# The last stage of a four-stage network: where the preparation of the last 512 tokens is placed, and which engine makes the low parts of the split operands

## The chip, the cores and the metric

The kernel runs on one core of one Trainium2 chip. A core has five engines with instruction queues of their own that run in order: PE (matrix multiplications), DVE and ACT (elementwise work over 128 partitions), POOL (elementwise work too) and SP, which here only starts transfers. Engines wait for each other by semaphores. The metric is the device time of one execution in microseconds (us); lower is better. Times are medians of several runs. The profile is that of one execution.

## The reference

`x` has 2 x 1024 tokens of 128 features. Four residual stages follow each other, each on a normalised `x`: an attention with 16 heads of 8, a mixture of 8 experts with two chosen, a causal attention with 8 heads of 128, and a mixture of 16 experts with four chosen. The change touches only the last one:

```python
t = x * rsqrt(mean(x * x) + EPS) * scale
g = t @ gate_w.T + gate_b
vals, idx = top_k(g, 4);  w = softmax(vals)          # route[e]: the weight of expert e, 0 if not chosen
for each expert e of 16:
    h = t @ w1[e].T + b1[e]                          # 128 -> 256, even outputs are x_glu, odd ones x_lin
    s = min(x_glu, 7) * sigmoid(1.702 * x_glu) * (clip(x_lin, 7, 7) + 1)
    acc += route[e] * (s @ w2[e].T + b2[e])
return x + acc
```

The clip has equal bounds, so its factor is always 8 and only the even outputs are needed. All 16 experts are computed for all tokens, and the route weights (mostly zero) scale their results.

## The kernel before

The 2048 tokens are worked on as four chunks of 512 (`c` = 0 to 3), with features on the partitions: a tile is 128 x 512 float32. The first three stages fill the time up to about 877 us. The last stage is made of two generators, whose `yield`s mark the points where the builder may change over to other work.

`ffn1_front(c)` (L989 to L1036) is the preparation of one chunk, in 16 pieces: statistics and inverse roots on DVE, the normalised tokens `f1tt` and `f1xl` (L1004, eight DVE operations), an addition into `x` on POOL (L1008), a transposition on PE, a scaled copy on ACT (L1012), the split of the transposed tokens into two parts (`f1x`), the gate's matmuls (L1019), four rounds of top-4 on small DVE tiles (L550 to L560), an exponential on ACT (L1025), the normalised route weights (up to L570), their transposition, and a store of them to DRAM (L1034), from which they are later loaded back broadcast over the partitions.

`ffn1_back(c)` (L1038 to L1084) are the 16 experts of one chunk. For expert `e`:

- three matmuls make `p` in PSUM (`mm3`, L161: high by high, high by low, low by high part, for near float32 precision); `pu` has four buffers,
- ACT applies the activation, into `f` (L1063), of which there are five buffers,
- DVE takes the minimum and multiplies with the broadcast route weight `gb` (L1064, called the scaling below); `gb` comes by a transfer that SP starts (L1048) and has eight buffers,
- `split` makes two parts of `f` for the next matmul: the high part is a rounding cast on ACT (L158), the low part the difference `f` minus high part (L159), on POOL or on DVE, by the expert's number (L1069),
- seven experts behind (`LAG`), three matmuls add the expert's result to `y` in PSUM.

After the sixteenth expert, `y` is copied, transposed, added to `x` (`res`, L1082) and stored (L1083).

The low parts go to POOL where `d % 5` is 1 or 3: experts 1, 3, 6, 8, 11 and 13 of a chunk, 6 of 16. The preparation of the first three chunks lies in the stage before. That of the last chunk runs with the experts of chunk 0: one piece after each expert (L1185). Chunk 1 follows alone, then chunks 2 and 3.

The order in which this program is written is not yet the order on the engines. Outside a part of the first stage the framework lays the instructions out with a planner, which walks a timeline with its own costs and reorders within each engine's queue; so the preparation's small DVE operations are found between the scalings of the experts, and some of them earlier or later than written. The final queues are fixed when the program is built, and each engine runs its queue in order. In the queues of this kernel, the eight normalisations of chunk 3 stand behind the scaling of expert 9 of chunk 0 on DVE, its top-4 rounds begin before the scaling of expert 15 of chunk 0, and its last small operation (L570) stands behind the scaling of expert 0 of chunk 2. POOL's addition (L1008) stands between the low parts of experts 8 and 11 of chunk 0.

Of the kernel before, what the change touches and what calls it, by code (L numbers as in the profile page):

```python
# [38 lines left out]
def cols(t, w=128):  # L39
    return slice(t * w, (t + 1) * w)  # L40


def run(*gens):
    for g in gens:
        for _ in g:
            pass
# [26 lines left out]
class Net:  # L73
# [964 lines left out]
    def ffn1_back(self, c, wk, pu, out):  # L1038
        nc = self.nc
        E = 16  # L1040
        LAG, PO = 7, (1, 3)
        F7 = 7.0 / (1.0 + math.exp(-1.702 * 7.0))
        xh, gT, gd = self.f1st.pop(c)
        gbs = []

        def bcast(e):
            gb = wk.tile([128, CH], F32, tag="f1gb", name=f"f1gb_{c}_{e}", bufs=8)
            nc.sync.dma_start(out=gb, in_=gd[e : e + 1, :].to_broadcast([128, CH]))  # L1048
            gbs.append(gb)

        for e in range(4):
            bcast(e)
        y = self.psy.tile([128, CH], F32, tag="y", name=f"f1y_{c}")
        nc.tensor.matmul(y, lhsT=self.f1b2, rhs=gT, start=True, stop=False)
        hs = []
        for e in range(E + LAG):
            if e + 4 < E:
                bcast(e + 4)
            if e < E:
                p = pu.tile([128, CH], F32, tag="u", name=f"f1p_{c}_{e}")  # L1060
                self.mm3(p, [w[:, e, :] for w in self.f1w1], xh)
                f = wk.tile([128, CH], F32, tag="f", name=f"f1f_{c}_{e}", bufs=5)
                nc.scalar.activation(f, p, AF.Gelu_apprx_sigmoid, bias=self.f1b1[:, e : e + 1])  # L1063
                nc.vector.scalar_tensor_tensor(f, f, F7, gbs[e], ALU.min, ALU.mult)  # L1064
                hs.append(f)
            d = e - 1
            if 0 <= d < E:
                fs = [wk.tile([128, CH], F32R, tag=f"fs{k}", name=f"f1s{k}_{c}_{d}", bufs=8) for k in range(2)]
                self.split(fs, hs[d], nc.gpsimd if d % 5 in PO else nc.vector)  # L1069
                hs[d] = fs  # L1070
            d = e - LAG
            if d >= 0:
                self.mm3(y, [w[:, d, :] for w in self.f1w2], hs[d], start=False, stop=d == E - 1)
            yield
        yT = wk.tile([128, CH], F32, tag="f1yT", name=f"f1yT_{c}")
        nc.scalar.copy(yT, y)
        yield
        tp = self.pt([128, TPC, D], f"f1ytp_{c}")
        for t in range(TPC):
            nc.tensor.transpose(tp[:, t, :], yT[:, cols(t)], self.ident)  # L1080
        res = self.tok.tile([128, TPC, D], F32, tag="xl", name=f"res_{c}")
        nc.vector.tensor_add(res, self.x[c], tp)  # L1082
        nc.sync.dma_start(out=out[c], in_=res)  # L1083
        yield  # L1084


def interleave(main, *sides, ratio=1):
    s = Side()
    for g in sides:
        s.add(g)  # L1090
    for _ in main:
        s.step(ratio)
    s.drain()


def held(net, gen):
    while True:
        with ExitStack() as ctx:
            for ins in net.marks.values():
                ctx.enter_context(net.tc.issue_after(ins.ins))  # L1100
            if next(gen, gen) is gen:
                return
        yield


def later(gen, n):
    for _ in range(n):
        yield
    yield from gen


def build(tc, aps, upto=4):
    n = Net(tc, aps)
    out = aps["out"].rearrange("(c t p) d -> c p t d", p=128, t=TPC)

    def dump():
        for c in range(NCHUNK):
            tc.nc.sync.dma_start(out=out[c], in_=n.x[c])

    with ExitStack() as ctx:  # L1120
        n.setup(ctx)
        c1 = ctx.enter_context(ExitStack())
        cr = ctx.enter_context(ExitStack())
        n.f0wp = n.pool(cr, "f0w")
        w1 = n.attn1_weights(c1)
        with ExitStack() as c0:
            cb = c0.enter_context(ExitStack())
            n.attn0(
                c0, cb,
                {170: lambda: n.ffn0_front(0), 270: lambda: n.ffn0_front(1), 266: lambda: w1,  # L1130
                 394: lambda: n.ffn0_front(2)}
                if upto > 1 else {},
            )
        if upto == 1:
            return dump()
        n.attn1_pools(c1)
        xh = [n.attn1_x(0), None]
        first, g = n.attn1_proj(0, 0, xh[0])
        n.f0k = n.pool(cr, "f0k", 1)
        gens = {"proj": islice(g, 5)}  # L1140
        for c in range(NCHUNK):
            gens[f"front{c}"] = n.ffn0_front(c)
            gens[f"up{c}"] = n.ffn0_up(c)
            gens[f"down{c}"] = n.ffn0_down(c)
        for i in range(2):
            gens[f"a1{i}"] = n.attn1_front(0, xh[0], i)
        with ExitStack() as c0:
            n.psu = n.pool(c0, "f0u", 4, PSUM)
            for word in ORDER.split():
                count, k = word.split("*")  # L1150
                for _ in range(int(count)):
                    next(gens[k], None)
            for k in gens:
                if k not in ("front0", "front1", "front2"):
                    run(gens[k])
            n.psu = None
            n.early = False
        with ExitStack() as c2:
            with ExitStack() as c3:
                n.a1s = n.pool(c3, "a1s", 3, PSUM)  # L1160
                n.a1o = n.pool(c3, "a1o", 1, PSUM)

                def front1():
                    xh[1] = n.attn1_x(1)
                    yield from n.attn1_front(1, xh[1], 0)
                    yield from n.attn1_front(1, xh[1], 1)

                def weights1():
                    cr.close()
                    n.f1wp = n.pool(c2, "f1w")  # L1170
                    yield from n.ffn1_weights()

                plan = {10: [lambda: held(n, front1())]}
                if upto > 3:
                    plan[9] = [lambda: held(n, weights1())]
                    plan[18] = [lambda: n.ffn1_front(0)]
                    plan[21] = [lambda: n.ffn1_front(1)]
                    plan[30] = [lambda: later(n.ffn1_front(2), 3)]
                n.attn1(first, g, xh, plan)
            c1.close()  # L1180
            if upto == 3:
                return dump()
            wk1 = n.pool(c2, "f1k", 2)
            pu = n.pool(c2, "f1u", 4, PSUM)
            interleave(n.ffn1_back(0, wk1, pu, out), n.ffn1_front(3), ratio=1)  # L1185
            run(n.ffn1_back(1, wk1, pu, out))
            run(n.ffn1_back(2, wk1, pu, out), n.ffn1_back(3, wk1, pu, out))


def layout(inputs):  # L1190
# [63 lines left out]
```

## Time and profile before

| | us |
|---|---|
| median of three runs (lowest, highest) | 992.36 (988.16, 992.86) |
| the profiled execution's own time | 993.87 |
| its span, first to last instruction | 992.1 |
| busy over the span: PE, DVE, ACT, POOL | 951.8, 839.4, 597.3, 317.3 |
| first matmul of the last stage's experts begins at | 877.6 |
| first scaling (L1064), last low part (L159) begin at | 882.6, 985.2 |
| 64 scalings on DVE, median of one | 0.680 |
| 40 low parts on DVE, median of one | 0.681 |
| 24 low parts on POOL, median of one | 1.299 |
| 64 activations on ACT, median of one | 0.684 |
| 64 high parts (casts) on ACT, median of one | 0.621 |
| granted TensorE clock over the span | 0.964 |

A row of the profile's groups names a line, an engine, an operation and its tiles, written from output to input, with a count and durations in ns. DVE and ACT start the next operation a little before the last one's recorded end, so an operation of 0.68 us takes up about 0.60 us of its engine. A row of a timeline begins with the start and the duration; several equal instructions in a row are put together with an "x" count; in brackets stands how long the engine had been idle, and what ended that. `f1f` is the activation's tile, `f1s` the split's two parts, `f1p` and `f1y` the two matmuls' results, `f1gb` the route weights.

### The profile page before, as it was taken

The page shows a single profiled execution, that of the slowest core. Times are in us where ns is not written, and L with a number is a line of the kernel's source. Part 1 is how long each engine was busy: PE and PEld are TensorE (multiplying, and loading weights), DVE is VectorE, ACT ScalarE, POOL GpSimd, SP SyncE. Part 2 cuts the span into 40 slices and gives each one's busy share as a digit, 9 for nine tenths or more (in the row PEclk, how much of TensorE's full clock was granted, in tenths as well). Part 3 has the DMA queues.
Part 4 walks back from the last instruction along what each step waited for, and adds up shares of the span by engine and source line. Part 5 has one row for each costly group of instructions (what it writes and reads, how often), then busy time and mean ns, then how long its engine had stood idle before and what let it go on. Part 6 is the DMA issues. An engine that isn't in the chain of part 4 may idle for free.

```text
span 992.1 us, 17673 instructions
## 1 busy us (share of the span) xinstructions
PE 951.8 (96%) x6546; PEld 616.8 (62%) x6546; DVE 839.4 (85%) x1885; ACT 597.3 (60%) x1149; POOL 317.3 (32%) x402
## 2 busy tenths in 40 slices
PE   5999999999999999999989999999999999998997
PEld 4643444444444434447767887788778789876675
DVE  7879789999988888526788897989999978989886
ACT  3157778888887776864435455444444544477775
POOL 7000300000010000002546557554645555336332
PEclk8989899999998978979999999999999999999999
DMA  5520231000200000013100001000000001144462
GB/s 171 191 75 2 99 116 55 2 2 22 80 20 26 2 1 2 2 33 118 44 2 12 22 12 54 23 12 12 12 1 24 12 13 33 33 142 156 151 192 74
DMA packets 33640, 50.94 MB, mean 51 GB/s; under 512 B 5141, under 2 KB 11250, under 8 KB 33554
## 3 DMA queue, kind: packets, MB, share of 16 engines
q1 hardware_dynamic: 33042, 49.68, 15.7%
q8 instruction: 51, 0.84, 0.3%
q14 instruction: 35, 0.29, 0.1%
q0 software_dynamic: 512, 0.13, 0.1%
HBM read 40.00 MB, written 9.67 MB: 50 GB/s over the span
## 4 chain that ended last, share of the span: by engine, by line
PE 62%; DVE 28%; ACT 4%; issue 4%; DMA 1%; SPq 1%; POOL 1%; DVEq 0%; ACTq 0%; POOLq 0%
PE av L415 9%; DVE mx L362 9%; PE o L878 8%; PE st L395 8%; PE st L845 7%; PE av L422 3%; PE s L804 3%; PE st L852 3%; PE f1y L163 2%; PE hot L474 2%; DVE pm L810 2%; PE f1p L163 2%; PE f0y L674 2%; PE s L357 2%; DVE pt L855 2%
## 5 line engine op out<-in xcount | busy, mean ns | idle before, releaser
L362 DVE TENSOR_REDUCE mx<-s 128x2 f32<-128x1024 f32 x256 | 301.5, 1218 | 33.5 <-PE s L357 29.0
L401 ACT ACTIVATE pt<-st 128x512 f32<-128x512 f32 x472 | 253.9, 598 | 69.3 <-PE s L357 54.6
L415 PE MATMUL av<-pt,V 128*32 128x256 f32 x2048 | 170.6, 414 | 0.0
L357 PE MATMUL s<-KS,QM 24*128 24x512 f32 x512 | 154.9, 511 | 7.2 <-DVE mx L362 5.3
L395 PE MATMUL st<-QM,KS 25*128 25x512 f32 x472 | 154.8, 511 | 3.8 <-ACT pt L401 2.3
L878 PE MATMUL o<-V,pt 128*128 128x129 f32 x1152 | 156.8, 277 | 0.3 <-ACT pt L857 0.3
L878 PEld LDWEIGHTS o<-V,pt 128*128 128x128 f32 x1152 | 146.7, 191 | 12.4 <-issue 3.9
L845 PE MATMUL st<-Q,K 128*128 128x512 f32 (+1 forms) x480 | 133.2, 389 | 5.5 <-DVE rB_q L747 3.6
L395 PEld LDWEIGHTS st<-QM,KS 25*128 25x128 f32 x472 | 66.9, 187 | 101.1 <-ACT pt L401 45.6
L857 ACT ACTIVATE pt<-pt 128x512 f32<-128x512 f32 x92 | 53.9, 592 | 73.8 <-DVE pt L855 73.8
L810 DVE TENSOR_REDUCE pm<-s 128x1 f32<-128x512 f32 (+3 forms) x160 | 80.8, 522 | 16.9 <-PE s L804 16.1
L845 PEld LDWEIGHTS st<-Q,K 128*128 128x128 f32 x480 | 78.8, 189 | 17.4 <-DVE rB_q L747 4.9
L415 PEld LDWEIGHTS av<-pt,V 128*32 128x32 f32 x2048 | 43.9, 112 | 69.2 <-issue 66.6
L857 ACT ACTIVATE pt<-st 128x512 f32<-128x512 f32 x68 | 37.5, 551 | 66.3 <-PE st L852 56.0
L357 PEld LDWEIGHTS s<-KS,QM 24*128 24x128 f32 x512 | 64.9, 187 | 20.0 <-DVE mx L362 14.2
L448 POOL TENSOR_TENSOR x<-x,ov 128x128 f32<-128x128 f32 x16 | 7.6, 472 | 194.5 <-DVE ov L443 194.5
L804 PE MATMUL s<-K,Q 128*128 128x512 f32 (+2 forms) x192 | 66.8, 380 | 1.1 <-DVE m L816 1.0
L891 POOL TENSOR_TENSOR x<-x,w 128x128 f32<-128x128 f32 x128 | 59.5, 465 | 24.9 <-ACT w L889 20.6
L855 DVE TENSOR_TENSOR pt<-st,mb 128x512 f32<-128x512 f32 x92 | 57.5, 632 | 5.1 <-PE st L845 1.3
L163 PE MATMUL f1y<-f1s,f1w 128*128 128x512 f32 x192 | 55.9, 412 | 5.1 <-POOL f1s L159 3.0
L889 ACT ACTIVATE w<-o,rz 128x128 f32<-128x128 f32 x128 | 39.9, 364 | 34.6 <-DVE rz L885 26.8
L377 POOL DMA_DIRECT2D QM<-mts x16 | 9.5, 592 | 158.4 <-ACT mts L376 157.7
(224 smaller groups left out, 1636.8 us busy)
## 6 DMA issues: line engine op xcount, KB each, us to landing
f1gb<-f1gd SPq DMA_DIRECT2D x64, 256.0 KB, 3.6
mb<-md SPq DMA_DIRECT2D x17, 256.0 KB, 3.2
f0gb<-f0gd SPq DMA_DIRECT2D x32, 128.0 KB, 3.0
qd<-q SPq DMA_DIRECT2D x12, 256.0 KB, 3.0
kd<-k SPq DMA_DIRECT2D x12, 256.0 KB, 3.0
QM<-qd SPq DMA_DIRECT2D x3, 1024.0 KB, 5.7
KS<-kd SPq DMA_DIRECT2D x2, 1024.0 KB, 6.8
KS<-kd SPq DMA_DIRECT2D x2, 768.0 KB, 8.0
```

Source lines behind the costliest of these rows:

```text
L163: self.nc.tensor.matmul(out, lhsT=lhs[l], rhs=rhs[r], start=start and i == 0, stop=stop and i == 2)
L357: self.last_s = nc.tensor.matmul(ps[:, k, :], lhsT=QM[c][r, g, cols(t)], rhs=KS[c // 2][r, g, cols(h, CH)], start=True, stop=True)
L362: self.marks["V"] = nc.vector.tensor_reduce(mxs[n][:, h, 2 * pr : 2 * pr + 2, t : t + 1], ps, AX.X, ALU.max, negate=True)
L395: nc.tensor.matmul(ps, lhsT=KS[c // 2][32 * j : 32 * j + 25, g, cols(kt)], rhs=QM[c][32 * j : 32 * j + 25, g, :], start=True, stop=True,)
L401: self.marks["A"] = nc.scalar.activation(e, ps, AF.Exp, scale=INV_SQRT_D)
L415: return nc.tensor.matmul(avs[n][cols(j, 32), q], lhsT=V[c // 2][kt // 4][:, kt % 4, 4 * g + j, :], rhs=es[j][:, q], start=kt == 0 and i = ...
L804: nc.tensor.matmul(s[:, 0 : k1 - k0], lhsT=Q[0][:, h, cols(qt)], rhs=K[0][:, k0:k1], start=True, stop=True)
L810: nc.vector.tensor_reduce(pm, s[:, 0:w], AX.X, ALU.max)
L845: k = nc.tensor.matmul(o, lhsT=K[l][:, cols(kt)], rhs=Q[r][:, :, q0 : q0 + w], start=i == 0, stop=apart and i == 2)
L855: nc.vector.tensor_sub(e[:, :, 256 - w :], o, mv)
L857: k = nc.scalar.activation(e[:, :, 256 - w :], o, AF.Exp, scale=INV_SQRT_D)
L878: nc.tensor.matmul(acc[t][:, h, :], lhsT=e[:, h, cols(t)], rhs=V[:, kt, h, :], start=(kt == 0 and h == 0), stop=(kt == qt and h == 1),)
```

## The change

Two edits, both in the last stage. The low parts alternate: those of the odd experts go to POOL, those of the even ones stay on DVE (8 and 8 of 16 in each chunk). And the preparation of chunk 3 no longer takes one piece per expert of chunk 0, but one piece after every third step of chunks 0 and 1; both have 25 steps, so the 16 pieces are used up in chunk 1 (`run` at the end finds none left).

```diff
     def ffn1_back(self, c, wk, pu, out):
...
-        LAG, PO = 7, (1, 3)
+        LAG = 7
...
-                self.split(fs, hs[d], nc.gpsimd if d % 5 in PO else nc.vector)
+                self.split(fs, hs[d], nc.gpsimd if d % 2 else nc.vector)
...
-            interleave(n.ffn1_back(0, wk1, pu, out), n.ffn1_front(3), ratio=1)
-            run(n.ffn1_back(1, wk1, pu, out))
-            run(n.ffn1_back(2, wk1, pu, out), n.ffn1_back(3, wk1, pu, out))
+            front3 = n.ffn1_front(3)
+            for c in range(2):
+                for k, _ in enumerate(n.ffn1_back(c, wk1, pu, out)):
+                    if k % 3 == 2:
+                        next(front3, None)
+            run(front3, n.ffn1_back(2, wk1, pu, out), n.ffn1_back(3, wk1, pu, out))
```

In the queues of the changed program, the eight normalisations of chunk 3 stand behind the scaling of expert 8 of chunk 0, its top-4 rounds begin before the scaling of expert 9 of chunk 1, and L570 stands behind the scaling of expert 2 of chunk 2. POOL's addition L1008 stands between the low parts of experts 7 and 9 of chunk 0. The addition of chunk 0's result (L1082) moves ahead, from behind the scaling of expert 4 of chunk 2 to behind that of expert 7 of chunk 1; its store (L1083), on SP, moves from behind the load of `gb` for expert 12 of chunk 2 to ahead of the first load for chunk 2. The store of chunk 3's route weights (L1034) moves from behind the load for expert 12 of chunk 2 to behind that for expert 14.

## The prediction

> **What bounds the kernel now.** The change lies in the last stage, so I read that stage alone. First the busy time by stretch, cut where the chain of work that ended last changes hands: up to about 940 us it runs mostly over DVE instructions, after that almost wholly over PE matmuls (columns: length, then busy time and count of PE, weight loads, DVE, ACT, POOL, then granted clock, DMA share, GB/s).
>
> ```profile
> 882.60:939.90 57.30, 53.26 (x227) 40.26 (x225) 54.77 (x111) 43.94 (x76) 26.52 (x14) 0.97 0.52 168
> 939.90:985.90 46.00, 44.68 (x181) 32.35 (x181) 40.34 (x51) 35.27 (x61) 15.77 (x12) 1.00 0.48 150
> ```
>
> The first stretch (experts of tokens 0 to 1023, with the preparation of the last 512 tokens between them) has DVE busy 96%. The second has it busy 88%, and there PE is the bound: its timeline has no gap over 0.1 us from 942.5 to 982, at 0.233 us per matmul. So the first stretch is priced by DVE, the second by PE, and the last split by itself.
>
> Second, the groups by tile (minimum/median/maximum ns) and the waits (total us, times, longest).
>
> ```profile
> L159 DVE TENSOR_TENSOR f1s<-f1f,f1s x40: 676/681/1782, 884.8 to 985.2; 128x512 fp32r<-128x512 f32 x40
> L159 POOL TENSOR_TENSOR f1s<-f1f,f1s x24: 1278/1299/2080, 885.3 to 982.7; 128x512 fp32r<-128x512 f32 x24
> ```
>
> ```profile
> DVE f1f L1064 <- ACT f1f L1063: 6.7, 11, 1.1
> ACT f1f L1063 <- POOL f1s L159: 4.1, 2, 3.1
> PE f1y L163 <- POOL f1s L159: 3.0, 2, 2.2
> ```
>
> Third, the timelines of POOL and DVE laid side by side.
>
> ```profile
> 888.07 1.50 POOL L159 TENSOR_TENSOR f1s<-f1f,f1s 128x512 fp32r<-128x512 f32 x1 [1.48 <-ACT f1s L158]
> 898.39 7.01 POOL L1008 TENSOR_TENSOR x<-x,f1xl 128x512 f32<-128x512 f32 x1 [1.26 <-PE f1tp L167]
> 905.37 2.95 POOL L159 TENSOR_TENSOR f1s<-f1f,f1s 128x512 fp32r<-128x512 f32 x2
> 957.93 1.29 POOL L159 TENSOR_TENSOR f1s<-f1f,f1s 128x512 fp32r<-128x512 f32 x1 [1.88 <-ACT f1s L158]
> ```
>
> ```profile
> 887.74 0.68 DVE L159 TENSOR_TENSOR f1s<-f1f,f1s 128x512 fp32r<-128x512 f32 x1
> 888.34 1.25 DVE L125 SCALAR_TENSOR_TENSOR rw_f<-rw_f,f1v 128x8 f32<-128x8 f32 x1
> 902.99 0.68 DVE L159 TENSOR_TENSOR f1x<-f1T,f1x 128x512 fp32r<-128x512 f32 x1
> 903.59 0.68 DVE L159 TENSOR_TENSOR f1s<-f1f,f1s 128x512 fp32r<-128x512 f32 x1
> 958.47 1.90 DVE L1064 SCALAR_TENSOR_TENSOR f1f<-f1f,f1gb 128x512 f32<-128x512 f32 x2 [0.50 <-ACT f1f L1063]
> ```
>
> A 128x512 DVE operation occupies 0.60 us (902.99 to 903.59; 0.68 with its tail). An 8-column operation that takes 0.15 us at 893.78 takes 1.25 us at 888.34, and ends (889.59) when POOL's split ends (889.57). At 958.47 two operations take 1.90 in place of 1.28, until after POOL's end at 959.22. So while a POOL operation reads SBUF, DVE stands still. It also goes the other way: POOL's addition at 898.39 needs 1.27 us (its twin for the tokens before took that), but takes 7.01, because DVE's operations run back to back past it.
>
> **The price of a split.** On DVE a split costs DVE 0.60 us. On POOL it costs DVE what it is held. I add up, over the first stretch, by how much DVE's instructions across each of the 13 POOL operations exceed their usual time: 1.14, 1.17, 1.10, 0.98, 0.70, 1.13, 0.36, 1.10, 1.00, 0.77, 1.17, 0.85, 1.17 = 12.6 us, 0.97 each; where DVE had no gap it is about 1.1. In the second stretch 12 POOL operations hold it 9.0 us, 0.75 each, because POOL often starts while DVE waits for ACT anyway. The Trainium skill (SBUF — State Buffer, Who interferes with whom) states the rule that speaks against the change: DVE instructions with two SBUF inputs and GpSimd instructions that read SBUF take a port by an exclusive lock, and the second to issue is blocked until the first is done. By the rule the price is POOL's whole 1.28 us, against 0.6 saved: 0.7 lost per moved split; by the rows it is 0.97 to 1.1, 0.4 to 0.5 lost. By the rule POOL would wait for one DVE instruction; the row at 898.39 shows it waiting past nine. I take the rows.
>
> **Part 1, low parts alternate.** Per 512 tokens 8 of 16 splits go to POOL in place of 6 (experts 1, 3, 6, 8, 11, 13 become all odd ones): 32 in place of 24.
> First stretch, 4 splits moved: DVE saves 4 x 0.60 = 2.4 and is held 4 x 1.1 = 4.4 more: +2.0. Bounds: 4 x 0.65 (every one beside idle DVE) gives +0.2, 4 x 1.28 gives +2.7.
> Second stretch, 4 moved: PE needs 12 x 0.233 = 2.79 us for two experts. DVE needs two scalings and a split, 1.8, and is held once, 0.75 to 1.17: 2.55 to 2.97. At the low end PE hides it (0), at the high end DVE becomes the bound and 14 pairs lose 0.18 each, 2.5. The cover is DVE's idle time, 6 us of 46. I take the middle, +1.2.
> The end: the split of expert 15 of the last tokens goes from DVE (0.68) to POOL (1.28), and nothing is behind it but three matmuls, the copy, the transposes and the store: +0.6, all on the path.
>
> **Part 2, the preparation.** It is the same work; every instruction is still issued: some 60 small DVE operations, on ACT the scaling, the cast, an exponential with two table loads of 1.28 and a copy, 12 small PE operations, POOL's addition L1008, one store on SP. What moves is its place in the orders. On DVE the eight normalisations move one expert earlier, the top-4 rounds start ten experts later (after the scaling of expert 8 of the second 512 tokens) but end at nearly the same place: the last operation (L570) stands behind scaling 2 of the third tokens, before it was behind scaling 0. So the first stretch holds the same sum of small operations: 0. The result addition of the first 512 tokens, 0.6, moves out of the second stretch into the first: +0.6. The table loads move from cast 4 to cast 11 of the second tokens; DVE waited 1.14 for them at 920.5 and will do so again: 0. On SP the store of the gates (L1034) moves behind two more loads, with some 15 us until those tokens' first scaling: 0. The store of the first result now stands ahead of the loads of the third tokens; it waits for an addition that DVE does before the scaling which frees the first of those buffers, so it adds its issue of 0.39 behind a wait: 0; if the result were late, every gate load behind it would be late too.
> POOL's L1008 stays between two splits, but now splits of experts 9, 11, 13 and 15 are queued behind it, and f has five buffers (L1062): the activation of expert 14 waits for split 9. DVE has seven large operations, 4.2 us, before it needs that activation. If L1008 is passed over again for these, then L1008 1.28, split 9 1.28, activation 0.69 and hand-overs of 0.25 leave DVE idle for 3.5 us, where the account above had two holds, 1.9: +1.6; split 11 then runs inside that idle time, holding DVE 0.4 and not 1.1: -0.6. Net +1.0; bounds 0 (not passed over) and +1.6. The PE stall of 2.19 that L1008 caused (907.13, followed by matmuls at a clock of 0.87) is no gain if it goes: DVE, not PE, set the end of that stretch.
>
> **Sum.** 2.0 + 1.2 + 0.6 + 0.6 + 1.0 = +5.4. The profiled execution took 993.87 (span 992.1 and 1.8 around it), so 999.3 there; on the median of the three runs, 992.36, it is 997.8. I forecast 997.8, own range 994.5 to 1001.
>
> **The rivals.** Lock-bound throughout: all 17 POOL operations of the first stretch hold 1.17 (19.9 against 12.6: +7.3), less 2.4, plus 0.6; the second at its upper end, +2.5; end +0.6: +8.6, 1001.0. For it speaks that the full holds are all where DVE has no gap; against it the mean of 0.97.
> Hidden: the four new holds are 0.65 each (+0.2), 0.6 for the result addition, PE covers the second stretch, end +0.6, L1008 free: +1.4, 993.8. For it: 0.62 to 0.70 is the common hold after 950.
> Faster: strict alternation puts POOL's split beside DVE's wait for ACT also in the first stretch. Then 17 holds of 0.65 are 11.0 against 12.6, -1.6; splits -2.4; result +0.6; two thirds of its 2.2 us of idle DVE go, -1.5; end +0.6: -4.3, 988.1. It decides when the hold falls below 0.6 to 0.7 us. Against it: DVE idles only 2.2 of 57 us there, so there is nearly no wait to lie beside.
>
> **How the numbers follow.** Forecast 0.45, lock-bound 0.22, hidden 0.15, faster 0.18. A measurement of this kernel tells about 0.5% (5 us) from no change. The forecast's case is past that in two thirds (0.29) and inside in one (0.16); lock-bound is slower (0.22); hidden is inside (0.13, 0.01 to each side); faster is past it in 0.14, inside in 0.04. Slower 0.52, same 0.33, faster 0.15. The range, 988 to 1003, spans all four and leaves out the outer parts of the two extremes.
>
> **What the profile after would show.** POOL 32 splits of median 1.3 with holds of about 1.1 in DVE's rows up to 940: right if the first stretch is 2 to 4 us longer. L1008 again far over 1.3 us with a DVE wait of 3 us behind ACT: the queue step. PE without gaps from there to the last tokens: the second stretch hidden. A POOL split as the last before the result: the end. Wrong, if the holds are mostly near 0.65, or if PE gaps, not DVE, set the first stretch.

## The result and the profile after

The changed kernel takes 995.82 us (median of 22 executions, 984.41 to 1002.52); the kernel before, measured in turns with it, 990.63 (22 executions, 979.71 to 994.74). The ratio is 1.0067, with a 95% interval of 1.004 to 1.0093: slower by 0.4 to 0.9%. (The ratios here leave out the executions that took over 1.5% more than the fastest of the same kernel, the profiled one of all_dve among them, so they are not just the quotients of the medians.) The prediction was a ratio of 997.8 / 992.36 = 1.0054.

One execution differs from another of the same kernel by up to 15 us (18 in the changed kernel), and the profiled execution of the changed kernel, 988.02 with a span of 986.3, lies at the low end of its times. Its first three stages, which the change leaves alone, ended 11.5 us earlier than in the profile of before (first scaling at 871.08 in place of 882.59). So I do not compare spans. What I compare in all that follows is **the length of the last stage**, from the start of the first scaling to the start of the last result addition, both on DVE. The kernel before, profiled twice, gives 105.46 and 105.19, and the changed kernel, profiled twice, 111.07 and 111.03: this length repeats to 0.3 us. The change costs 5.6 us in the stage it touches, which is 0.57% of 990.63.

First the busy time of the changed kernel by stretch, with the columns of the prediction's first table. The cut is the same operation in both kernels, scaling 3 of the third tokens; for the kernel before these two stretches are 57.28 and 48.18 us long, with DVE busy 54.75 and 40.38.

```profile
871.08:933.18 62.10, 55.01 (x225) 40.95 (x223) 58.22 (x107) 44.88 (x76) 30.79 (x18) 0.95 0.52 163
933.18:982.15 48.97, 45.37 (x188) 33.15 (x188) 38.63 (x47) 35.33 (x62) 21.30 (x15) 1.00 0.41 130
```

The first stretch grew by 4.82, and DVE is still busy 94% of it. The second grew by 0.79. Then the groups by tile and DVE's wait in the last stage of the changed kernel, in the columns of the prediction:

```profile
L159 DVE TENSOR_TENSOR f1s<-f1f,f1s x32: 675/680/1779, 873.2 to 977.9; 128x512 fp32r<-128x512 f32 x32
L159 POOL TENSOR_TENSOR f1s<-f1f,f1s x32: 1269/1470/1837, 873.8 to 978.7; 128x512 fp32r<-128x512 f32 x32
```

```profile
DVE f1f L1064 <- ACT f1f L1063: 7.5, 9, 1.9
```

POOL has its 32 splits, and they take a median of 1.470 us where the 24 of before took 1.299: POOL, too, waits for DVE more often. DVE's wait behind the activation grew from 6.7 to 7.5 in all, and its longest from 1.1 to 1.9. Where these lie is seen in the timelines of POOL and DVE:

```profile
886.87 4.59 POOL L1008 TENSOR_TENSOR x<-x,f1xl 128x512 f32<-128x512 f32 x1 [2.63 <-PE f1p L163]
891.43 2.95 POOL L159 TENSOR_TENSOR f1s<-f1f,f1s 128x512 fp32r<-128x512 f32 x2
895.53 1.74 POOL L159 TENSOR_TENSOR f1s<-f1f,f1s 128x512 fp32r<-128x512 f32 x1 [1.16 <-ACT f1s L158]
...
907.11 1.27 POOL L159 TENSOR_TENSOR f1s<-f1f,f1s 128x512 fp32r<-128x512 f32 x1 [1.64 <-ACT f1s L158]
...
931.09 1.27 POOL L159 TENSOR_TENSOR f1s<-f1f,f1s 128x512 fp32r<-128x512 f32 x1 [3.31 <-ACT f1s L158]
```

```profile
890.43 1.58 DVE L159 TENSOR_TENSOR f1s<-f1f,f1s 128x512 fp32r<-128x512 f32 x1
893.89 1.64 DVE L1064 SCALAR_TENSOR_TENSOR f1f<-f1f,f1gb 128x512 f32<-128x512 f32 x2 [1.88 <-ACT f1f L1063]
...
896.07 2.35 DVE L1064 SCALAR_TENSOR_TENSOR f1f<-f1f,f1gb 128x512 f32<-128x512 f32 x2
...
907.15 1.77 DVE L1064 SCALAR_TENSOR_TENSOR f1f<-f1f,f1gb 128x512 f32<-128x512 f32 x1
...
931.15 1.77 DVE L1064 SCALAR_TENSOR_TENSOR f1f<-f1f,f1gb 128x512 f32<-128x512 f32 x1
```

At 907.15 and 931.15 a scaling that takes 0.68 takes 1.77, while POOL's split beside it takes its plain 1.27: a hold of 1.09. Added up as the excess of each DVE operation over its usual time, the 18 POOL operations of the first stretch hold DVE 1.11, 1.11, 1.10, 0.97, 0.90, 0, 0.36, 1.07, 1.10, 0.71, 1.11, 1.09, 1.10, 1.11, 1.10, 1.09, 1.10, 1.09 = 17.2 us. Counted in this way the 13 of before come to 12.3; the prediction has 12.6. At 886.87 the addition L1008 is again passed over by DVE, for 3.3 us this time; the splits of experts 9 and 11 follow it at 891.43, and DVE waits 1.88 for an activation that needs the buffer of split 9.

### The profile page after: what moved, and what is told of

Read it like the earlier page. It is cut to its first block, busy times and chain, and to the rows that moved or that the text cites. A ratio compares the mean times of both kernels' runs of the same rounds, so it can differ in the third digit from the quotient of the medians.

```text
span 986.3 us, 17681 instructions
## 1 busy us (share of the span) xinstructions
PE 942.8 (96%) x6546; PEld 614.0 (62%) x6546; DVE 838.8 (85%) x1877; ACT 597.4 (61%) x1149; POOL 326.6 (33%) x410
## 4 chain that ended last, share of the span: by engine, by line
PE 58%; DVE 29%; ACT 5%; issue 5%; DMA 2%; POOL 1%; SPq 0%; POOLq 0%; DVEq 0%; ACTq 0%
DVE mx L362 10%; PE av L415 9%; PE o L878 9%; PE st L395 8%; PE st L845 7%; PE s L804 3%; PE av L422 3%; PE st L852 3%; DVE pm L810 2%; PE f0y L674 2%; DVE pt L855 2%; ACT pt L401 2%; PE hot L474 1%; PE s L357 1%; DVE rB_q L746 1%
## 5 line engine op out<-in xcount | busy, mean ns | idle before, releaser
L415 PE MATMUL av<-pt,V 128*32 128x256 f32 x2048 | 166.0, 404 | 0.1
L159 POOL TENSOR_TENSOR f1s<-f1f,f1s 128x512 fp32r<-128x512 f32 x32 | 47.5, 1488 | 56.0 <-ACT f1s L158 46.9
```

The costliest lines, as they stand in the source:

```text
L415: return nc.tensor.matmul(avs[n][cols(j, 32), q], lhsT=V[c // 2][kt // 4][:, kt % 4, 4 * g + j, :], rhs=es[j][:, q], start=kt == 0 and i = ...
```

## The experiments

All lengths of the last stage are from one profile each. A dash: one time only, no interval.

| kernel | stage, us | to before | first stretch, second | timed ratio to before, 95% |
|---|---|---|---|---|
| before | 105.46 | | 57.28, 48.18 | |
| before_again | 105.19 | -0.3 | 57.02, 48.17 | - |
| the changed kernel | 111.07 | +5.6 | 62.10, 48.97 | 1.0067, 1.004 to 1.0093 |
| after_repeat | 111.03 | +5.6 | 62.01, 49.02 | - |
| alternate_alone | 112.94 | +7.5 | 63.31, 49.63 | 1.0114, 1.0051 to 1.0177 |
| spread_alone | 106.83 | +1.4 | 59.53, 47.30 | 1.0017, 0.9989 to 1.0045 |
| extra_read | 114.07 | +8.6 | 62.53, 51.54 | - |
| extra_write | 105.19 | -0.3 | 58.40, 46.79 | - |
| after_add_dve | 110.36 | -0.7 to the changed | 61.42, 48.94 | - |
| after_last_dve | 110.24 | -0.8 to the changed | 61.89, 48.35 | - |
| all_dve | 104.36 | -1.1 | 48.07, 56.29 | 1.001, 0.9983 to 1.0037 |
| dve_ordered_a | 96.67 | -8.8 | 55.81, 40.86 | 0.9956, 0.9917 to 0.9995 |
| dve_ordered_c | 100.10 | -5.4 | 56.62, 43.48 | 0.9969, 0.9922 to 1.0017 |
| dve_ordered_add | 97.20 | -8.3 | 56.33, 40.87 | 0.9939, 0.9889 to 0.9988 |

### The yardstick: before_again and after_repeat

Both kernels unaltered.

> The kernel before, unchanged, to see how far one profile of the last stage can be trusted. The measure is the length of the last stage: from the start of the first scaling (L1064) to the start of the last result addition (L1082), 105.46 us before and 111.07 us after the change. If the stage repeats within 1 us, the difference of 5.6 us is the change's; if it moves by 3 us or more from run to run, single profiles can't carry the parts.

> The changed kernel once more, unaltered, so that a difference of a few tenths in its last stage can be trusted. The last stage, from the first scaling to the last result addition, took 111.07 us in the first profile. If that length belongs to the order of the queues, it comes out between 110.8 and 111.4, although the whole execution may differ by 10 us. If it is as scattered as the whole time, it differs by more than 1 us, and the differences of the other stages say little.

Measured: 105.19 and 111.03, where the first profiles have 105.46 and 111.07, in executions of 987.22 and 993.03 us. The stage's length belongs to the order of its queues; the scatter of the total lies in the stages ahead of it. Differences above half a microsecond can be read. The granted clock over the stage was 0.98 and 1.00 in the two of before, 0.97 and 0.98 in the two of the changed kernel: it moved as much between two profiles of one kernel as between the kernels, and the length did not follow it.

### Each part alone: alternate_alone and spread_alone

```diff
-                self.split(fs, hs[d], nc.gpsimd if d % 5 in PO else nc.vector)
+                self.split(fs, hs[d], nc.gpsimd if d % 2 else nc.vector)
```

> Only the alternating low parts (8 of 16 to POOL); the preparation stays one piece per expert of the first 512 tokens. Theory (holds: each split moved to POOL stops DVE for about 1.1 us and saves it 0.6): stage 109 to 111 us, nearly the whole loss, and the holds in DVE's rows up to the last small operation of the preparation sum to about 17 us against 12.6. Rival (the moved preparation makes the loss): stage within 1.5 us of 105.5.

```diff
-            interleave(n.ffn1_back(0, wk1, pu, out), n.ffn1_front(3), ratio=1)
-            run(n.ffn1_back(1, wk1, pu, out))
-            run(n.ffn1_back(2, wk1, pu, out), n.ffn1_back(3, wk1, pu, out))
+            front3 = n.ffn1_front(3)
+            for c in range(2):
+                for k, _ in enumerate(n.ffn1_back(c, wk1, pu, out)):
+                    if k % 3 == 2:
+                        next(front3, None)
+            run(front3, n.ffn1_back(2, wk1, pu, out), n.ffn1_back(3, wk1, pu, out))
```

> Only the preparation spread over the experts of 1024 tokens; low parts of experts 1, 3, 6, 8, 11, 13 on POOL as before. Theory (the same DVE work, one result addition of 0.6 us more ahead of the end of the preparation): stage 105.5 to 107 us. Rival (the moved preparation makes the loss): stage 109 to 111 us.

Measured: the alternation alone costs 7.5 us of the stage (112.94, above the 109 to 111 expected) and, in four executions, 0.5 to 1.8% of the time. The spreading alone costs 1.4 in its profile, and its interval contains 1. Together they cost 5.6 and not 8.9, so the two do not add: beside the alternation the spreading saves 1.9 us, where alone it costs 1.4. How the alternation alone loses its time is seen in the busy times of its first stretch, in DVE's waits there (in total us, times, longest), and in the row of the longest:

```profile
879.38:942.69 63.31, 56.86 (x230) 42.50 (x228) 54.46 (x108) 45.81 (x79) 29.62 (x18) 0.92 0.48 156
```

```profile
DVE f1f L1064 <- ACT f1f L1063: 6.4, 4, 3.1
DVE f1g L1021 <- PE f1lg L1019: 1.6, 1, 1.6
```

```profile
901.73 1.03 DVE L1064 SCALAR_TENSOR_TENSOR f1f<-f1f,f1gb 128x512 f32<-128x512 f32 x1 [3.10 <-ACT f1f L1063]
```

DVE is busy no longer than before (54.46, before 54.75), and its holds in this stretch, counted as above, are 12.8 us; up to the preparation's last operation, for which about 17 was expected, they are 12.0. What grew is its idle time, 8.85 us in place of 2.53. So in this kernel the loss comes through waits and not through holds; while DVE waits, a split on POOL has little to stop.

In the kernel before, the first of these waits is 2.2 us in that stretch and the second is absent; in the changed kernel it is 3.4, and the second is absent too. With the preparation still close together, the splits of the odd experts stand behind the passed-over L1008 (5.19 us here), DVE waits 3.10 for the activation, and the gate's matmuls come late as well. Spread over two chunks, the same queue makes DVE wait 1.88 and the gate's result is there in time. What the spreading improves is thus a wait that the alternation brings, and most of it comes back as holds: DVE's idle time falls from 8.85 to 3.88, its holds rise from 12.8 to 17.2.

### What a hold costs by itself: extra_read and extra_write

In the first, POOL makes the low parts of experts 5 and 10 of every chunk a second time, into a tile that nothing reads; DVE keeps all of its work. In the second, POOL instead fills the used-up tile of these experts with zeros, twice. Eight extra reads, or 16 fills, in the stage; the outputs are the same.

```diff
                 self.split(fs, hs[d], nc.gpsimd if d % 5 in PO else nc.vector)
+                if d in (5, 10):
+                    idle = wk.tile([128, CH], F32, tag="idle", name=f"idle_{c}_{d}", bufs=1)
+                    nc.gpsimd.tensor_sub(idle, hs[d], fs[0].bitcast(F32))
```

> The kernel before, and for experts 5 and 10 of each 512 tokens POOL makes the low part a second time into a tile that nobody reads; DVE keeps all its work. So POOL has the 32 differences of the changed kernel and DVE saves nothing: this is the price of a hold alone. Theory (holds): 4 more holds of 1.1 us in the first stretch (+4.4), 4 more of 0.75 in the second, mostly hidden by PE; stage 109 to 111.5 us. Rival (POOL's work is free for DVE, and the loss comes from the other order): stage within 1.5 us of 105.3.

```diff
+                if d in (5, 10):
+                    for _ in range(2):
+                        nc.gpsimd.memset(hs[d], 0.0)
```

> The kernel before, and after the low part of experts 5 and 10 of each 512 tokens POOL fills the used-up activation tile twice with zeros: POOL operations at about the same places that write SBUF and read none. Theory (the hold comes from POOL's reads of SBUF against DVE's second input): DVE's rows across these fills keep 0.60 us each, and the stage is within 1.5 us of 105.3. Rival (any POOL operation stops DVE): stage 1.5 to 4 us longer, and DVE's rows across a fill are longer by the fill's time.

Measured: 114.07 and 105.19. Eight operations of POOL whose result nobody waits for lengthen the stage by 8.6 us, 1.08 each; 16 that only write lengthen it by nothing. For the reading kernel the group with who waited for it (total us, times), and the stretches:

```profile
L1072 POOL TENSOR_TENSOR idle<-f1f,f1s x8: 1260/1473/2441, 886.2 to 979.3; 128x512 f32<-128x512 f32 x8
...
ACT f1f L1063: 3.3, 1
```

```profile
877.85:940.38 62.53, 55.55 (x230) 41.67 (x228) 58.19 (x112) 45.45 (x78) 33.03 (x18) 0.95 0.50 159
940.38:991.92 51.54, 47.04 (x184) 33.51 (x183) 44.09 (x50) 34.79 (x60) 22.54 (x15) 0.97 0.41 127
```

Against the kernel before, DVE's busy time grew by 3.44 and 3.71, with four reads in each stretch and not one DVE instruction more in the stage (one split of 0.60 has gone from the second stretch to the first): 7.15 us of holds, 0.89 per read. The other 1.5 us are waits. So 1.08 is not the price of a hold by itself: a read keeps a buffer of `f` longer, and one activation waits 3.3 us for an added read to be done with its buffer. The planner also moved some operations by a place or two, L570 among them. The total is above the upper end of what I had put on it; in the second stretch PE hides less than I thought, for the stretch grew by 3.4 us. For the writing kernel, POOL and then DVE across two of the fills and a split:

```profile
891.95 1.11 POOL L1072 MEMSET f1f<- 128x512 f32 x2 [0.70 <-DVE rw_f L125]
893.22 1.36 POOL L159 TENSOR_TENSOR f1s<-f1f,f1s 128x512 fp32r<-128x512 f32 x1 [0.15 <-ACT f1s L158]
```

```profile
891.80 0.68 DVE L1064 SCALAR_TENSOR_TENSOR f1f<-f1f,f1gb 128x512 f32<-128x512 f32 x1
...
892.48 0.68 DVE L1064 SCALAR_TENSOR_TENSOR f1f<-f1f,f1gb 128x512 f32<-128x512 f32 x1
...
893.34 1.32 DVE L1004 TENSOR_SCALAR f1xl<-x,mv_f,rs_f 128x128 f32<-128x128 f32 x1
```

The two scalings keep their 0.68 us beside the fills; a normalisation beside POOL's split of 893.22 takes 1.32 in place of 0.34. It is POOL's reading that stops DVE, not POOL's being at work. The unchanged length is a sum, though: with the fills between them the splits meet DVE elsewhere, DVE is busy 92.6 us of the stage in place of 95.1, and idle that much longer. The rule of the Trainium skill that the prediction weighed (SBUF — State Buffer, Who interferes with whom) says the same of the scaling, a DVE instruction with two SBUF inputs: it excludes a GpSimd instruction that only writes.

### Two terms of the sum: after_add_dve and after_last_dve

Both start from the changed kernel. The first takes L1008 of the last 512 tokens to DVE, the second the very last split.

```diff
-        nc.gpsimd.tensor_add(x, x, xl)
+        (nc.vector if c == 3 else nc.gpsimd).tensor_add(x, x, xl)
```

> The changed kernel with the one addition of the last 512 tokens (L1008) on DVE. The prediction priced its place in POOL's queue at +1.0 us. If that price is right, the stage comes back by 1.0, to 110.1. By the rows of the changed kernel it is less: the addition costs DVE 0.6, DVE's wait of 1.88 behind the activation and the addition's hold of 0.90 go, but the splits of experts 9 and 11, which held DVE 0 and 0.36 because it was waiting, hold it 1.1 each: 0.6 - 1.88 - 0.90 + 1.1 + 0.74 = -0.3, a stage of 110.7. If the PE wait of 3.64 us at 893.18 is what counts, the stage comes back by 2 to 3.6, to 107.5 to 109.

```diff
-                self.split(fs, hs[d], nc.gpsimd if d % 2 else nc.vector)
+                self.split(fs, hs[d], nc.gpsimd if d % 2 and (c, d) != (3, 15) else nc.vector)
```

> The changed kernel with the last split of all, of expert 15 of the last tokens, on DVE as before. Every queue is otherwise the same. The prediction puts +0.6 on this: the stage comes out 0.6 to 0.7 shorter, 110.4, and the time from the start of the last cast to the copy of the result is 2.2 in place of 2.8. If the copy or the weights of the last matmuls are late for another reason, it stays at 2.8 and 111.1.

Measured: without L1008 on POOL the stage is 0.7 us shorter, and the rows are not what either reading expected. POOL and DVE of that kernel:

```profile
891.58 6.02 POOL L159 TENSOR_TENSOR f1s<-f1f,f1s 128x512 fp32r<-128x512 f32 x2 [2.44 <-ACT f1s L158]
```

```profile
897.11 1.64 DVE L1064 SCALAR_TENSOR_TENSOR f1f<-f1f,f1gb 128x512 f32<-128x512 f32 x2 [1.88 <-ACT f1f L1063]
```

Two splits that take 2.95 behind L1008 in the changed kernel now take 6.02: DVE passes over the split of an expert in L1008's place, and the wait of 1.88 is still there. So the wait does not belong to the addition; a split that meets DVE's back-to-back run at that place brings the same. What the move gave back, 0.7, is near one hold of about 1.1 less 0.6 of work for DVE; this is argued, not shown, for the planner also moved other operations (the split of the transposed tokens, the start of the top-4 rounds and a result addition by one expert).

With the last split on DVE the stage is 0.8 shorter, and the end is what it was before. ACT's last cast and the copy of the result, in the changed kernel and then in this one:

```profile
978.01 0.62 ACT L158 CAST f1s<-f1f 128x512 fp32r<-128x512 f32 x1 [0.84 <-DVE f1f L1064]
980.82 0.58 ACT L1076 COPY f1yT<-f1y 128x512 f32<-128x512 f32 x1 [2.19 <-PE f1y L163]
```

```profile
975.67 0.62 ACT L158 CAST f1s<-f1f 128x512 fp32r<-128x512 f32 x1 [0.83 <-DVE f1f L1064]
977.84 0.58 ACT L1076 COPY f1yT<-f1y 128x512 f32<-128x512 f32 x1 [1.55 <-PE f1y L163]
```

From the start of the cast to the start of the copy: 2.81 and 2.17 us (before: 2.16).

### The other direction: all_dve

If POOL's splits cost more than they save, none of them on POOL should be best.

```diff
-                self.split(fs, hs[d], nc.gpsimd if d % 5 in PO else nc.vector)
+                self.split(fs, hs[d])
```

> The kernel before with every low part on DVE, none on POOL; the preparation as before. Theory (holds): in the first stretch DVE gains 12 splits of 0.6 (7.2 us) and loses some 11.5 us of holds, -4.3; in the second DVE needs 2.4 us for two experts against PE's 2.79, so nothing is lost; stage about 101 us, some 4 us shorter than before, though DVE has 24 operations more. Rival (POOL unloads DVE, and the loss came from queueing at POOL): 12 more operations in the stretch that DVE bounds, +7, stage 111 to 113 us.

Measured: a ratio of 1.001 (0.9983 to 1.0037), no gain. The stage is 104.36 and not about 101. Up to 960 there is a gain, and a large one: the first stretch takes 48.07 us, partly because the end of the preparation has left it. Then it is lost again. Busy time by stretch, then DVE and PE around 965:

```profile
883.24:960.00 76.76, 76.41 (x339) 60.10 (x338) 69.07 (x152) 64.34 (x109) 4.61 (x1) 1.00 0.48 149
960.00:965.00 5.00, 0.81 (x2) 0.00 (x0) 0.69 (x1) 0.00 (x0) 0.00 (x0) 0.79 0.61 195
965.00:987.60 22.60, 19.93 (x73) 15.24 (x73) 19.50 (x32) 16.79 (x28) 0.00 (x0) 0.82 0.48 178
```

```profile
965.57 1.35 DVE L1064 SCALAR_TENSOR_TENSOR f1f<-f1f,f1gb 128x512 f32<-128x512 f32 x2 [3.25 <-DMA f1gb<-f1gd]
```

```profile
966.96 2.37 PE L163 MATMUL f1y<-f1s,f1w 128*128 128x512 f32 x4 [6.15 <-ACT f1s L158]
```

PE is busy 76.41 of 76.76 us, then has nothing for 6.15: DVE waits for the route weights of the last 512 tokens. The planner had put the end of their preparation (L570) at 952.46, where the kernel before has it at 937.42, and the store and the loads come after it. For the next six microseconds a matmul takes about 0.43 us (three from 969.13 to 970.41) in place of 0.233, and the granted clock over the rest is 0.82. The holds were gone, and the order that the planner made gave the gain back.

### A version that beats both: dve_ordered_a, dve_ordered_c, dve_ordered_add

All low parts on DVE, and the preparation held to its place: each scaling of the first three chunks is issued after the preparation's last written DVE operation, and the 16 pieces are spread over three chunks. The first two differ in the spacing only.

```diff
-                nc.vector.scalar_tensor_tensor(f, f, F7, gbs[e], ALU.min, ALU.mult)
+                with ExitStack() as ctx:
+                    if c < 3:
+                        ctx.enter_context(self.tc.issue_after(self.prep.ins))
+                    nc.vector.scalar_tensor_tensor(f, f, F7, gbs[e], ALU.min, ALU.mult)
...
-                self.split(fs, hs[d], nc.gpsimd if d % 5 in PO else nc.vector)
+                self.split(fs, hs[d])
...
-            interleave(n.ffn1_back(0, wk1, pu, out), n.ffn1_front(3), ratio=1)
-            run(n.ffn1_back(1, wk1, pu, out))
-            run(n.ffn1_back(2, wk1, pu, out), n.ffn1_back(3, wk1, pu, out))
+            front3 = n.ffn1_front(3)
+            for c in range(3):
+                for k, _ in enumerate(n.ffn1_back(c, wk1, pu, out)):
+                    if k % (3, 4, 4)[c] == 2:
+                        next(front3, None)
+            run(front3, n.ffn1_back(3, wk1, pu, out))
```

(`self.prep` is set at L1004, at L558 and L560 and at L570; in dve_ordered_c the condition is `k % (3, 2, 2)[c] == 1`.)

> All low parts on DVE, and the preparation of the last 512 tokens spread over the experts of the 1536 tokens before (each third step of the first 512, each fourth after), with the planner told to place each piece before the scaling that follows it in the program. In the kernel with all low parts on DVE, PE ran without gaps until it waited 6.15 us for the last tokens' route weights, whose top-4 rounds the planner had put off to the end of the third tokens, and then ran at half speed for 4 us. Theory (without holds PE is the bound, and only the late weights cost): stage 95.5 to 99 us, some 7 us under before (ratio about 0.993). Rival (DVE can't carry all low parts and the preparation in time): stage 103 us or more.

> As the one before, but with a piece at each second step of the second and third tokens, so the top-4 rounds come sooner and closer together. Theory: DVE is short of time in the second 512 tokens (8 scalings and low parts of 0.6 and two rounds of about 1.2 us against PE's 5.6 us for four experts), so PE has gaps there that the other spacing has less of: stage 96 to 100.5 us. Rival as before: 103 us or more.

The third is dve_ordered_a with L1008 of these tokens on DVE, as in after_add_dve.

> The kernel of dve_ordered_a with the addition L1008 on DVE too, so that POOL does nothing in the last stage for these tokens. In dve_ordered_a the stage took 96.67 us with PE almost without a gap: 416 matmuls at 0.2325 are 96.7. If PE is the bound there, taking the last hold of 1.1 us off DVE changes nothing: 96.4 to 97.0, and a ratio of about 0.995 to the kernel before. If DVE were still the bound, the stage would be 0.5 shorter or more, below 96.2.

Measured: 981.51 against 988.6 of the kernel before (0.9956, 0.9917 to 0.9995), 984.51 (0.9969, not told apart from 1) and 979.83 against 987.69 (0.9939, 0.9889 to 0.9988). The first by stretch, and the longer of the only two PE waits over 0.3 us between 881 and 977 (the other is 0.36 at 935.62):

```profile
881.35:937.16 55.81, 55.32 (x240) 41.91 (x239) 53.49 (x123) 47.44 (x81) 4.62 (x1) 1.00 0.58 185
937.16:978.02 40.86, 39.73 (x173) 30.77 (x171) 36.11 (x60) 32.63 (x57) 0.00 (x0) 1.00 0.46 149
```

```profile
940.91 1.67 PE L163 MATMUL f1y<-f1s,f1w 128*128 128x512 f32 x6 [0.42 <-DVE f1s L159]
```

PE is busy 95.05 of 96.67 us at full clock: the stage is bound by its matmuls, 8.8 us shorter than before, with all 64 low parts on DVE. L1008 is passed over here as well (4.62 us), and costs nothing: dve_ordered_add without it is 97.20, no shorter. The closer spacing of dve_ordered_c, which was to leave fewer gaps, is 3.4 us longer than dve_ordered_a; the cause is open. No run holds the preparation to its place with splits still on POOL, so how much of the 8.8 us is the order's own is not shown. The timed gain of dve_ordered_a, 0.44%, is smaller than 8.8 us would be, 0.89%; the interval reaches to 0.83%, and dve_ordered_add's to 1.1%. What its true size is stays open.

## Why the prediction was right, step by step

The direction and the size were right: +5.4 forecast, +5.6 in the stage and 1.0067 in the timed runs. By the account of the changed kernel the mechanism was right too; the parts, run alone, show that it is not the only one. "Lock-bound throughout" (+8.6), "hidden" (+1.4) and "faster" (-4.3) did not come about. The terms:

- **The price of a split.** The prediction took the rows, about 1.1 us where DVE has no gap, over the rule's 1.28. 13 of the 18 POOL operations of the changed kernel's first stretch hold DVE between 1.07 and 1.11, and in extra_read an added read holds it 0.89 on the mean over both stretches (1.08 with the waits that it brings). A split on DVE costs 0.60, so moved to POOL beside a busy DVE it costs 0.5 more. Shown. The prediction's sums of the holds before are a little high: counted as in the changed kernel, 12.3 and not 12.6 in the first stretch, 8.3 and not 9.0 in the second. And "DVE stands still" is too wide, as the last section shows.
- **First stretch.** Forecast +3.6, its own sign 2 to 4, measured +4.82. The difference lies mostly in where I cut. The hold of the split of expert 1 of the third tokens lies behind the cut in the kernel before (at 939.87, 0.62 over the usual 0.68) and ahead of it in the changed kernel (at 931.15, 1.09); taken out, the stretch grew by 3.7. By account: 4 splits less on DVE -2.4, holds +4.9, the result addition +0.6 (it is there, at 908.85), idle time 3.88 in place of 2.53, +1.35; these make 4.45, and 0.4 I cannot assign.
- **The queue of L1008, +1.0.** This step is the one that was sized wrongly. Passing over, the buffers running out and the DVE wait behind the activation came as described, but the wait is 1.88 and not 3.5. The prediction had all seven of DVE's large operations pass over L1008 and let DVE stand idle from the moment it lets L1008 in; only six passed, and DVE still had the seventh, a split, to do at 890.43, which with its hold of 0.90 fills 1.58 of the 3.5 and leaves 1.92, an estimate from these figures. Split 9 held nothing, as forecast, and split 11 0.36. Wait 1.88, less the hold of 1.0 of split 9 and 0.6 of split 11 at the mean price, is +0.3. And it is no property of L1008: after_add_dve has the same 1.88 with a split in its place. The 3.5 us were nearly met by alternate_alone, 3.10, where the preparation is dense. So the price belonged to the alternation under the old placing, and I charged it to the new one.
- **Second stretch, +1.2.** Measured +0.14 without the end; with the 0.6 of the hold that went over the cut +0.8, inside the bounds of 0 and 2.5. PE still hides most: its longest waits there are 0.94 and 0.86.
- **The end, +0.6.** Measured 0.64 from cast to copy; undone, 0.8 of the stage came back. Shown.
- **The preparation, 0.** Alone, the spreading costs 1.4 in its profile (0.6 of it forecast for the result addition) and a ratio that cannot be told from 1. With the alternation it saves 1.9. The prediction priced the two parts as if they added; they do not, because holds and waits take each other's place: the alternation alone has DVE idle 8.85 us and held 12.8 in its first stretch, the changed kernel idle 3.88 and held 17.2.

The lucky part: the smaller queue step, the 0.4 unassigned and the sum of the two stretches nearly cancel. In the changed kernel the holds carry the result; that is so under its placing of the preparation. Under the old placing the same alternation loses more, and by waits in the first stretch, which grows by 6.0 of the 7.5: had the change been the alternation alone, 2.0 + 1.2 + 0.6 + 1.0 = 4.8 of the prediction's terms would have stood against the measured 7.5.

## What to carry to other kernels

Before moving elementwise work with SBUF inputs from a busy DVE to POOL, compare what DVE saves with what POOL's reads stop it for: here 0.60 against 1.1 us per 128x512 operation where DVE had no gap, so "more balanced" was slower, and the best kernels had no split on POOL at all. Count waits beside holds: a queue behind a passed-over POOL operation can cost as much as the holds. But taking a cost away can let a planner move something else late: all_dve gained nothing until the preparation was also held to its place. Where the total scatters by 10 us, measure the length of the stage that was changed; it repeated to 0.3 us.

## What the runs showed that I had not expected

- DVE passes a waiting POOL operation by for many instructions: L1008 took 7.01 us in the kernel before, 7.02, 7.03 and 7.08 in before_again, extra_read and extra_write, 4.59 in the changed kernel, where its plain time is 1.27. At 895.53 a split was let in after one DVE instruction. What decides between the two stays open.
- POOL's fills, 16 of 0.53 us each, beside DVE cost the stage nothing, its eight added reads 8.6 us.
- Two edits of one stage did not add: +7.5 and +1.4 alone, +5.6 together. In its first stretch the first loses by waits when alone, by holds when together.

Which DVE operation a POOL read stops depends on what that operation reads. In the kernel before, L1008 gets in for its last 1.27 us, from 904.13 to 905.40; a reduction with one SBUF input begins inside that time and keeps its usual 0.2 us, while a copy, also with one input, takes 1.32 in place of 0.18 beside the split of 912.36:

```profile
904.44 0.22 DVE L550 TENSOR_REDUCE tk_f<-f1g 128x4 f32<-128x64 f32 x1
...
912.94 1.32 DVE L558 COPY tk_f<-tk_f 128x64 f32<-128x64 f32 x1
```

In all profiled kernels together, the seven reductions that begin well inside a POOL read (taken as the last 1.27 us of its row) keep their time, and so do two result additions with one input in PSUM (0.68, in extra_read and extra_write). The scalings and low parts that begin there, with two inputs in SBUF, are longer without exception.
